# Splitting one step of a token sort in two, in a one-core decoder kernel whose work is interleaved by a planner

## Chip, core and metric

The kernel runs on one core of a Trainium2 chip. The metric is device microseconds of one execution of the whole program; the median of three runs stands for a kernel. A profile is one further execution, recorded by the hardware profiler, with a time of its own.

## What is computed

One decoder layer over x, 4 batches of 512 tokens by 512 channels, in three residual parts:

```
x = x + mamba(layernorm(x))          # in_proj, conv, selective scan over 512 positions, out_proj
x = x + quant_ffn(layernorm(x))      # two int8-style linears, weights given per batch
x = x + moe(layernorm(x))            # 16 experts, each token uses its best 2, and a shared expert
```

The part that is changed belongs to the experts. A router picks two experts for each token; the result is `combine`-weighted:

```
topw, sel = top_k(softmax(x @ gate_w.T), 2)
hmid = silu(einsum('th,eih->tei', x, w1)) * einsum('th,eih->tei', x, w3)
moe_out = einsum('tei,ehi->th', hmid * combine[:, :, None], w2)
```

The kernel does not compute all 16 experts for all tokens. It sorts the tokens by expert into tiles of 128 rows and computes each tile with its one expert.

## The kernel before, in words

**The long work.** The selective scan is cut into 256 units (4 batches of 64), called slots here, counted from 1. `scan_batch` writes one after another. A unit is an exponential on ScalarE (L724), a product on GpSimd (L726), the scan on VectorE (L733) and a product on VectorE (L739, tile `h`, five buffers); TensorE sums `h` over states every few units (L751, into `py`), and VectorE gates the sum (L773).

**The work beside it.** Everything else is written as Python generators that `yield` what their next step needs: an engine's name, a tile, or a condition. `Steps` wraps a generator, and `Pace` keeps a rough plan of when each engine will be free and each tile written. Three times in each unit `more` goes through the generators and lets each do at most two steps; a step is done only if `Pace.clear` agrees. For a step that names PE, the planned end of TensorE's queue may be at most 5,000 ns (`BEHIND`) behind VectorE's, and the tile it names may be ready at most 3,500 ns (`SLACK`) late, each plus the `rest` that the place allows. A bare `yield` names only VectorE and nearly always passes. So a `yield` decides where the instructions after it stand in the engines' queues. The queues themselves are in order: an instruction that waits holds what stands behind it.

**The generators in the last batch of the scan** (slots 193 to 256) are:

- `backs`: for each batch in turn out_proj with its residual (L806, L816), the two quantised linears (transposes and maxima L913, L918; scaling products L963, L974, L1011; products L1081, L1087), and `moe_front`: router (L1197 to L1232) and shared expert (L1147, L1139 up and gate, L1162, then L1171, L1177). Batch 3's part can only start once the scan has ended.
- `routed`, that is `experts` for group 0 (batches 0 and 1): `sort`, then `expert_tiles`.
- after the scan, `last`, which is `experts` for group 1 (batches 2 and 3). From there on the loop at the end of `run` takes the step whose operands the plan has ready first, with 2,000 ns (`FIRST`) in favour of `backs`, or of `last` once the router of batch 3 is done and until its tiles have begun.

**The sort.** T is 8 blocks of 128 tokens, NS is 31 tile places. After counts and positions (L1366 to L1439) a list of token numbers by place is made by products: for each of four pairs of blocks, VectorE writes 0/1 operands `at_r` (L1446) and `at_s` (L1453, L1459), and TensorE adds four small products of them into one PSUM bank `pk` (L1466). After the fourth pair VectorE writes the list `tok` (L1471) and frees the bank. There are three such banks during the scan, a, b and g, for all generators together; eight after it.

**The tiles.** For each tile GpSimd issues two gathers, the rows `xs` (L1505, by `tok`) and the expert's weights `wx` (L1263, by `wrow`). TensorE transposes (L400), ScalarE copies (L1525), TensorE makes the two up-products (L1534), ScalarE and VectorE the gated activation (L1539, L411, L1542), TensorE the down-product (L1547), ScalarE copies (L1550) and SyncE stores the result to `y_d` (L1553). During the scan two tiles are loaded ahead, after it eight. The tiles of a group must be done before the weights of the next are fetched (the condition at L1422, before `first_weights`). At the very end GpSimd gathers `y_d` back by token (L1301), VectorE adds (L1311) and SyncE stores.

Of the kernel before, what the change touches and what calls it, by code (L numbers as in the profile page):

```python
# [46 lines left out]
PE, ACT, POOL, SP = "PE", "Activation", "Pool", "SP"  # L47
# [222 lines left out]
class Kernel:  # L270
# [1083 lines left out]
    def sort(self, sb, G, group, fixed, pos, tok, wrow, count, first_weights, few):  # L1354
# [89 lines left out]
        for t in range(0, T, 2):  # L1444
            at_r = sb.tile([P, 2, 2, P], F16, name="at_r", tag="xT", bufs=few)
            nc.vector.tensor_tensor(  # L1446
                at_r,
                iota_p.rearrange("p (a b q) -> p a b q", a=1, b=1).to_broadcast([P, 2, 2, P]),
                rm[:, t : t + 2, :].unsqueeze(3).to_broadcast([P, 2, 2, P]),
                ALU.is_equal,  # L1450
            )
            at_s = sb.tile([P, 2, 2, NS], F16, name="at_s", tag="ys", bufs=min(2 * few, 6) if few > 2 else few)
            nc.vector.tensor_tensor(  # L1453
                at_s,
                iota_s.rearrange("p (a b q) -> p a b q", a=1, b=1).to_broadcast([P, 2, 2, NS]),
                sl[:, t : t + 2, :].unsqueeze(3).to_broadcast([P, 2, 2, NS]),
                ALU.is_equal,
            )
            nc.vector.tensor_mul(  # L1459
                at_s,  # L1460
                at_s,
                tokf[:, t : t + 2].rearrange("p (a b q) -> p a b q", b=1, q=1).to_broadcast([P, 2, 2, NS]),
            )
            for j in range(2):
                for i in range(2):
                    nc.tensor.matmul(  # L1466
                        pk, at_r[:, j, i, :], at_s[:, j, i, :], start=(t + j + i == 0), stop=(t + j == T - 1 and i == 1)
                    )
            yield
# [338 lines left out]
```

## Time and profile before

| | |
|---|---|
| median of three runs | 1624.45 us (1622.11 to 1625.10) |
| the profiled execution | 1637.25 us, of which the recorded span is 1635.5 us |
| busy share of the span | PE 73%, VectorE 73%, GpSimd 67%, ScalarE 57% |
| mean granted TensorE clock | 0.849 |
| sort of group 0: first operand to `tok` | 1020.7 to 1048.8 us |
| last scan unit ends, its last sum on TensorE ends | 1331.3, 1338.0 us |
| sort of group 1: first operand to `tok` | 1474.8 to 1480.0 us |
| last product of TensorE begins | 1599.0 us |

The profiled execution is 12.8 us longer than the median of the others, so a sum of durations from the profile is set against 1637.25 us and a difference is then carried to the median. In a row of the timeline the columns are start, duration, engine, line, operation, tiles and shapes, and in brackets the idle time before it and what ended it. Each f32 product is recorded as two matmuls, so one line-L1534 step of a tile shows as x16.

### The profile page before, as it was taken

Reading aid. Unit: us, or ns where it says so; the run is one execution under the profiler, and the core shown is the slowest. Engines: PE = TensorE matmul, PEld = TensorE weight load, DVE = VectorE, ACT = ScalarE, POOL = GpSimd, SP = SyncE. Lnnn points to the kernel's source line nnn. Section 1 sums busy time; section 2 is a strip of 40 time slices with the busy share of each in tenths; the row PEclk is TensorE's granted clock in tenths of the full one; section 3 lists DMA queues with packets and bytes.
Section 4 is the critical chain, followed back from the end, with each engine's and each line's share of the span. In section 5 each row is a group of like instructions: output and inputs, shape, how many; then the busy total and the mean of one; then the engine's idle time right before and its main releaser. Section 6 shows DMA issues by size and latency. Waiting matters only on the chain. (4 is left out here: it accounts for less than half of the span.)

```text
span 1635.5 us, 15478 instructions
## 1 busy us (share of the span) xinstructions
PE 1201.9 (73%) x4552; PEld 586.3 (36%) x4552; DVE 1196.0 (73%) x1256; ACT 939.6 (57%) x1592; POOL 1095.3 (67%) x907
## 2 busy tenths in 40 slices
PE   6867877557865767899867885856666799867990
PEld 2222222112332323333423432334434346643670
DVE  4588899898857888788787888977788863453413
ACT  3386677755657778555797753367676413530240
POOL 1079899886768888677887965687878653017443
PEclk9978788768877887999878887888787999978996
DMA  5475555675233655666345559565556557258776
GB/s 200 146 180 128 132 107 118 126 180 119 87 84 73 136 118 157 176 180 166 84 98 118 159 123 280 154 181 129 152 143 186 147 190 258 78 194 304 288 301 233
DMA packets 106521, 262.19 MB, mean 160 GB/s; under 512 B 13056, under 2 KB 17280, under 8 KB 106368
## 3 DMA queue, kind: packets, MB, share of 16 engines
q1 hardware_dynamic: 93120, 204.50, 47.8%
q0 software_dynamic: 13312, 56.63, 9.7%
q8 instruction: 40, 0.66, 0.2%
q14 instruction: 49, 0.40, 0.1%
HBM read 153.87 MB, written 45.88 MB: 122 GB/s over the span
## 5 line engine op out<-in xcount | busy, mean ns | idle before, releaser
L726 POOL TENSOR_TENSOR bu<-bc,rep 128x1024 f32<-128x1024 f32 x256 | 602.0, 2358 | 181.9 <-DVE da L733 135.9
L733 DVE TENSOR_TENSOR_SCAN da<-da,bu 128x1024 f32<-128x1024 f32 x256 | 586.2, 2290 | 89.6 <-POOL bu L726 55.8
L724 ACT ACTIVATE da<-rep,a_sb 128x512 f32<-128x512 f32 x512 | 352.6, 690 | 248.9 <-DVE h L739 221.0
L739 DVE TENSOR_TENSOR h<-da,bc 128x1024 f32<-128x1024 f32 x256 | 312.1, 1219 | 19.4 <-PE py L751 9.1
L751 PE MATMUL py<-h,sel 128*32 128x512 f32 x1024 | 165.1, 683 | 47.7 <-DVE h L739 47.5
L502 POOL TENSOR_TENSOR u<-u,tap 128x511 f32<-128x511 f32 (+2 forms) x72 | 91.1, 1266 | 18.3 <-ACT tap L498 16.0
L446 PE MATMUL bank_a<-xnT,win 128*128 128x512 f32 x176 | 96.5, 699 | 8.9 <-ACT tap L498 6.1
L446 PE MATMUL bank_g<-xnT,win 128*128 128x512 f32 x184 | 89.5, 632 | 5.1 <-ACT tap L498 4.2
L751 PEld LDWEIGHTS py<-h,sel 128*32 128x32 f32 x1024 | 30.9, 117 | 157.8 <-issue 79.9
L1263 POOL DMA_INDIRECT wx<-in_wexp,wrow x48 | 48.9, 1020 | 55.8 <-PE bank L1547 12.3
L446 PE MATMUL bank_b<-xnT,win 128*128 128x512 f32 x120 | 61.1, 656 | 13.0 <-ACT sp_r L681 11.0
L446 PEld LDWEIGHTS bank_a<-xnT,win 128*128 128x128 f32 x176 | 39.1, 230 | 61.3 <-issue 50.1
L1505 POOL DMA_INDIRECT xs<-xn_d,tok x48 | 49.8, 1037 | 16.4 <-issue 14.7
L1301 POOL DMA_INDIRECT yg<-y_d,pos x32 | 32.0, 1002 | 37.3 <-DMA y_d<-ys 21.1
L446 PEld LDWEIGHTS bank_g<-xnT,win 128*128 128x128 f32 x184 | 36.1, 202 | 56.7 <-issue 43.4
L1534 PE MATMUL bank<-xT,wx 128*128 128x128 f32 x368 | 47.4, 284 | 6.7 <-issue 5.3
L695 POOL TENSOR_TENSOR sp_e<-sp_e,dd 128x512 f32<-128x512 f32 x31 | 39.4, 1272 | 16.7 <-ACT dd L690 16.5
L1534 PEld LDWEIGHTS bank<-xT,wx 128*128 128x128 f32 x368 | 45.0, 198 | 10.3 <-issue 8.3
L411 DVE SCALAR_TENSOR_TENSOR hs<-hs,bank 128x128 f32<-128x128 f32 x25 | 7.1, 282 | 52.2 <-ACT hs L1539 45.4
L446 PEld LDWEIGHTS bank_b<-xnT,win 128*128 128x128 f32 x120 | 24.9, 215 | 49.2 <-issue 30.3
L1539 ACT ACTIVATE hs<-bank 128x128 f32<-128x128 f32 x25 | 6.5, 275 | 62.7 <-PE bank L1534 31.5
L806 PE MATMUL bank_g<-wout,u 128*128 128x512 f32 x64 | 34.0, 692 | 10.3 <-ACT tap L498 6.2
(429 smaller groups left out, 2424.2 us busy)
## 6 DMA issues: line engine op xcount, KB each, us to landing
rep<-dd SPq DMA_DIRECT2D x128, 512.0 KB
win<-in_win SPq DMA_DIRECT2D x64, 256.0 KB
x<-xr SPq DMA_DIRECT2D x48, 256.0 KB
xr<-x SPq DMA_DIRECT2D x48, 256.0 KB
y_d<-ys SPq DMA_DIRECT2D x48, 256.0 KB
bc<-rows_d SPq DMA_DIRECT2D x32, 256.0 KB
gz_d<-gz SPq DMA_DIRECT2D x32, 256.0 KB
gzl<-gz_d SPq DMA_DIRECT2D x32, 256.0 KB
```

The source lines that it names most:

```text
L446: nc.tensor.matmul(pj, win[:, k, :], xnT[:, k, :], start=(k == 0), stop=(k == NK - 1))
L502: nc.gpsimd.tensor_add(u[:, j:], u[:, j:], v[j][:, j:])
L695: ew.tensor_sub(e, e, du)
L724: nc.scalar.activation(da[:, i, :], rep[:, i, 0, :], AF.Exp, scale=self.a_sb[:, q, g : g + 1])
L726: nc.gpsimd.tensor_mul(bu, st["bc"][0, g].unsqueeze(1).to_broadcast([P, NP, L]), rep[:, :, 1, :])
L733: self.nc.vector.tensor_tensor_scan(daf, daf, buf, 0.0, ALU.mult, ALU.add)
L739: self.nc.vector.tensor_mul(h, st["da"].pop((c, n)), st["bc"][1, g].unsqueeze(1).to_broadcast([P, NP, L]))
L751: nc.tensor.matmul(py[q * CH : (q + 1) * CH, :], self.sel, st["h"][c, g, q // NP][:, q % NP, :], start=False, stop=(g == NG - 1),)
L806: nc.tensor.matmul(po[t], st["u"][c][:, t * P : (t + 1) * P], wout[c], start=(c == part[0]), stop=(c == part[-1]),)
L1263: nc.gpsimd.indirect_dma_start(out=ws[s], out_offset=None, in_=self.wexp, in_offset=bass.IndirectOffsetOnAxis(ap=wrow[:, s : s + 1], axis= ...
L1505: nc.gpsimd.indirect_dma_start(out=xs[s], out_offset=None, in_=xn_d, in_offset=bass.IndirectOffsetOnAxis(ap=tok[:, s : s + 1], axis=0), bo ...
L1534: nc.tensor.matmul(ph[:, i, :], w[:, o : o + P], xT[:, k, :], start=(k == 0), stop=(k == NK - 1))
```

## The change

In the loop over the four pairs, one `yield` more is put between VectorE's operands and TensorE's products; the one after the products stays. The step that wrote both is now two, and the second is written only when the plan finds TensorE and `at_s` near enough. No instruction is added, removed or altered.

```diff
@@ sort, the loop "for t in range(0, T, 2)", after at_s is written
                 at_s,
                 tokf[:, t : t + 2].rearrange("p (a b q) -> p a b q", b=1, q=1).to_broadcast([P, 2, 2, NS]),
             )
+            yield PE, at_s
             for j in range(2):
                 for i in range(2):
                     nc.tensor.matmul(
```

## Prediction

> **What bounds the kernel now.** I read the page first, then the table of stages by windows, then the waits in the last batch of the scan, then TensorE's own timeline from the end of the scan on, because the change touches two places: a sort that runs beside the scan and one that runs after it. The columns of the windows are stage, length, then busy time and count for PE, PE's weight loads, VectorE, ScalarE and GpSimd, then the granted clock, the DMA share and GB/s.
>
> ```profile
> 1050.00:1338.00 288.00, 203.42 (x915) 113.23 (x913) 231.36 (x232) 171.78 (x301) 209.18 (x174) 0.85 0.55 152
> 1338.00:1444.00 106.00, 92.83 (x502) 63.90 (x502) 42.75 (x102) 45.88 (x99) 25.85 (x39) 0.95 0.50 180
> 1444.00:1480.00 36.00, 21.52 (x85) 14.98 (x86) 21.14 (x77) 8.02 (x12) 12.28 (x19) 0.67 0.65 237
> 1480.00:1526.00 46.00, 40.22 (x116) 20.17 (x116) 14.17 (x23) 3.30 (x7) 27.00 (x28) 0.89 0.82 290
> 1526.00:1600.00 74.00, 70.52 (x461) 54.96 (x459) 17.57 (x52) 29.12 (x67) 31.41 (x31) 1.00 0.78 291
> ```
>
> The first row is the scan beside everything else: VectorE is busy 231 of 288 us and sets the pace, with 57 us of holes. The other rows are the tail: from 1338 to 1444 and from 1526 to 1600 TensorE is the full engine (88% and 95%); the stage between, 1444 to 1480, is a chain of router and sort in which nobody is full. So work moved from the scan into the tail goes from a place where TensorE has 85 us free to one where it has few.
>
> The holes of the scan stage, in the view of who waited for whom (total us, times, longest), and in the groups of that window:
>
> ```profile
> DVE da L733 <- POOL bu L726: 14.9, 6, 5.7
> DVE wsc L974 <- PE bank_b L963: 7.7, 2, 7.4
> L400 PE MATMUL bank_a<-ident,xs 128*128 128x128 f32 x24 | 5.6, 378 | 32.1 <-DMA xs<-xn_d,tok 32.1
> ```
>
> TensorE stood 32.1 us before transposes of tiles whose rows had not come; once this reached VectorE as the 7.4 us hole before L974.
>
> **What the new order is.** The changed program's instruction order per engine can be read without running it. All engines have the same instructions; these stand elsewhere (slots counted as in the text above).
>
> 1. Group 0's sort. Before, the four pairs were written at slots 195, 195, 196, 196 and `tok` at slot 201. Now the first two pairs' operands stand at 195 and 196, and the other two at 204 and 205, because the plan sees the eight-product groups L806 queued on TensorE; `tok` follows at 206. By the starts of L733 (slot 201 at 1046.4 us, 206 at 1069.3) this is about 23 us later. Bank g is held five slots longer, so out_proj of batch 2 alternates a and b alone; its four sums L816 stay at 202, 202, 203, 204, so that costs nothing. What ended up behind: the first two row gathers on GpSimd go from after product 202 to after 207.
> 2. Tiles. The activation L1542 of tile 1 moves from slot 209 to 212, tile 7 from 225 to 235, tile 10 from 235 to 255. Before the scan ended 13 tiles had their L1542, now 10.
> 3. `backs` for batch 2: router from slot 240 to 245, and three of its four last products L1171 used to stand after the last `py` products but one and interleaved with units 254 to 256; now all four stand in one row right before the last L751.
> 4. Group 1's sort: one group L1139 that stood behind the four quads of L1466 now stands before them; on VectorE one L1162 stands before `tok`.
> 5. SyncE's stores L1553 and GpSimd's gathers move with their tiles. In the trace SyncE's queue waited 56 us at L1553 in this stage, in front of `rep` loads L711; with fewer stores there that can only ease, and GpSimd saw `rep` late for just 2.3 us, so I price it at nothing.
>
> **Part 1, the quads themselves.** VectorE's 12 operand instructions take 0.68 + 0.28 + 0.29 us per pair, 1.25 us, four times, before and after; only their slot changes. TensorE's quads take 0.27 us. Before, TensorE stood idle 10.86 us before the first quad with L806 behind it; the first quad is still there, and the second, 0.86 us of waiting, goes. Sum: 0 to -1 us, I take 0.
>
> **Part 2, end of the scan.** From the router of batch 2 to the last L751 TensorE still has in its queue: 12 groups L1147, L1139, L1171 of 3.44 us (start to start in the trace), 41.3; four L751 groups of 1.92, 7.7; three L1534 of 1.79, 5.4; two L1547, two L747 of 0.86, 3.4; two L400 of 0.44, 0.9. That is 58.7 us, nearly without holes since the L1171 wait only for each other's banks; with 3 us for those, 62 us. Before, the same stretch took from 1258.2 to 1338.0, 80 us, of which the five slots that no longer lie in it (L733 of slot 240 at 1255.1, of slot 245 at 1283.5, less the router's own 4.8 us on VectorE) are 24. So 56 us becomes 62: +6 us. Against it stand three tiles' VectorE work no longer in the scan, 3 x 0.57, -1.7 us. I take +4. Bounds: -8 if holes of the scan like the 7.4 us one vanish with the thinner tiles and no new ones come, +9 if new ones come. There is reason for one: the gather of tile 4 now stands behind product 220 on GpSimd and its transpose before the L751 for slots 217 to 220, with four L913 and a VectorE maximum of slot 221 behind; the trace shows 9.3 us from the issue of such a gather to its transpose.
>
> **Part 3, the tail up to 1444.** Of group 0's 24 tiles these steps lay after the last L751 before: 10 L400, 11 L1534, 11 L1547; now 13, 13 and 14. The steps' prices are the distances from start to start in these rows of TensorE's timeline:
>
> ```profile
> 1369.08 1.95 PE L1534 MATMUL bank<-xT,wx 128*128 128x128 f32 x16
> 1370.87 0.60 PE L400 MATMUL bank<-ident,xs 128*128 128x128 f32 x4
> 1371.30 1.88 PE L806 MATMUL bank_a<-wout_c,u 128*128 128x512 f32 x4
> 1373.02 1.02 PE L1547 MATMUL bank_b<-wx,hs 128*128 128x512 f32 x2
> 1373.88 1.02 PE L1547 MATMUL bank_g<-wx,hs 128*128 128x512 f32 x2
> ```
>
> 1.79, 0.43 and 0.86 us: 2 x 1.79 + 3 x 0.43 + 3 x 0.86 = 7.5 us more. Here a rule speaks otherwise. The Trainium skill, "Perfetto Trace Analysis", section "Identifying the Most-Contended Engine", says that matmul busy time misleads on TensorE, and that the share of weight loading tells its slack. That share is 63.9 of 106 us; by it 40% is free and the three tiles cost nothing. The rows decide otherwise: the next group starts exactly where the one before leaves off, whatever loads weights. What the rows do show free is the bracketed holes of the stretch up to the last tile at 1432, 7.5 us in six places, all before steps of the chain or of the tile itself. Not all can be filled, because the holes are waits of 0.6 to 1.9 us; I let tiles fill 3 us. So +4.5 us, between 0 and +7.5. ScalarE and VectorE have half their time free here. DMA moves 180 GB/s here and 290 later, so three tiles' weights find room.
>
> **Part 4, the second sort.** Rows of TensorE's timeline around it:
>
> ```profile
> 1460.26 5.11 PE L1147 MATMUL bank<-xnT,ws 128*128 128x512 f32 x8
> ...
> 1467.02 3.60 PE L1147 MATMUL bank_g<-xnT,ws 128*128 128x512 f32 x8
> 1476.08 0.29 PE L1466 MATMUL bank<-at_s,at_r 128*128 128x31 f16 x4 [5.46 <-DVE at_s L1459]
> 1477.20 0.27 PE L1466 MATMUL bank<-at_s,at_r 128*128 128x31 f16 x4 [0.82 <-DVE at_s L1459]
> ...
> 1479.59 5.69 PE L1139 MATMUL bank_b<-xnT,ws 128*128 128x512 f32 x8
> ```
>
> The hole of 5.46 us now takes an L1139, 3.44 us, which ends before the first `at_s` is there. TensorE's queue is then full from 1479.6 to 1598 as before, one group shorter: -3.4 us. `tok` gets one L1162 before it (0.69 us), but the row gathers stand behind eight weight gathers that GpSimd issues until 1482.7, so that is hidden. The clock could add to it: the L1139 after the holes took 5.69 us and not 3.60. The Trainium skill, "TensorE: Matmul & The Clock Gate", section "HAM oscillation", says that holes of over some 3.4 us let the clock fall; this hole shrinks to 2 us, which by the rule keeps it and saves 2.1 us more. But the granted clock in this stage is 0.67, and the 20 us of layernorm, router and sort around it stay sparse; I take nothing. Bounds -5.5 and 0.
>
> After 1600 nothing changes: sixteen gathers and the last store.
>
> **Sum.** 0 + 4 + 4.5 - 3.4 = +5.1 us on the profiled execution's 1637.25, 1642.3; carried to the median, 1624.45 + 5.1 = 1629.5 us.
>
> **Rivals.**
>
> - *Faster, because TensorE's queue is no longer held by late rows.* Thirteen tiles among the scan cost 32.1 us of TensorE in waits, about 7 us at a time; ten could cost two waits fewer, and each that reaches VectorE is a hole like the 7.4 us before L974. Two such holes less, -14, with parts 3 and 4 as above and +4 at the scan's end: 1624.45 - 14 + 4 + 4.5 - 3.4 = 1615.6. It decides from 6 us of vanished holes on. For it: the first two row gathers now have no L963 of the first linear that waits behind a late one. Against it: the pairs left are spaced just as closely to their transposes. 22%.
> - *No change.* The tail's holes take 6 us of the 7.5, and the scan's end is 2 us later: +2 + 1.5 - 3.4 = 0.1, 1624.6. 15%.
> - *Much slower.* A new hole of 4.5 us at slot 221, the scan's end +6, nothing filled in the tail, and no gain in the sort because bank or operands hold the L1139: 4.5 + 6 + 7.5 = +18, 1642.5. 18%.
> - That the change does nothing is excluded: the order of instructions differs on every engine from slot 196 on.
>
> **Chances.** The likeliest, +2 to +9 us (1626 to 1633), 45%. Within 0.2%, 3.2 us, lies what a measurement here can hardly tell from no change: all of the second rival but a little, and the lower seventh of the likeliest. So faster 0.24, same 0.20, slower 0.56. The range reaches to the faster rival and into the much slower: 1616 to 1645.
>
> **What would show it.** `tok` of group 0 some 20 us later; ten tiles' L1542 before the last L733; the last L751 ending 2 to 6 us later than 1338; 13 up-product groups between it and the second sort; an L1139 in the hole before the first late quad, and the stretch from `tok` to the last product 3 us shorter than 119 us. The prediction is wrong if the scan's end comes over 4 us earlier, that is if the holes of VectorE between 1050 and 1338 sum to well under 57 us, or if the tail from the last L751 to the second `tok` is not longer than its 142 us.

## The result, and the profile after

The changed kernel takes 1637.67 us (median of 12 runs, 1634.24 to 1643.03), the kernel before 1626.01 us in the runs beside it (12 runs, 1622.11 to 1631.79). The ratio is 1.0065, 95% interval 1.0053 to 1.0078: slower, by some 11 us. The prediction had +5.1 us; the sign is right, and 1637.67 lies in the range, but the difference is twice the one forecast. The profiled execution of the changed kernel took 1639.63 us, its span is 1637.9 us. Lines behind the added one are numbered one or two higher in the changed kernels: their L1535 is L1534 of the kernel before.

The two profiled executions differ by 2.4 us only, because that of before had holes on TensorE late in the tail that other profiles do not have (see the last section). For the same reason positions are compared from a common mark: the start of L733 of slot 193, which is the first unit of the last batch. It stands at 994.4 us before and at 993.5 us after. Both kernels were profiled twice.

| us after slot 193 | router L1197 of batch 2 ends | last L733 begins | last sum L751 ends | second list `tok` written |
|---|---|---|---|---|
| before | 263.8 | 334.6 | 343.6 | 485.6 |
| before, second profile | 265.2 | 335.1 | 344.0 | 486.1 |
| after | 277.1 | 336.9 | 354.4 | 504.0 |
| after, second profile | 278.3 | 336.1 | 353.6 | 503.1 |

The last unit of the scan begins 1 to 2 us later. Its last sum on TensorE ends some 10 us later, the second list comes 17 to 18 us later. Such positions vary by some us between executions: group 0's split alone (the first experiment), which has the changed kernel's order up to the second sort, had the last sum at 348.6 and the list at 498.7. From the list on, the last down-product L1547 begins 101.5 us later in both profiles of after. In two kernels that have before's order of work there, and were profiled without those holes (the first and the third experiment), it takes 106.4 and 106.1 us. So 4.6 to 4.9 of the 17 to 18 us come back, which leaves some 13 us where 11 were measured.

The same stretches as windows. First the kernel before; the columns are those of the table of stages (window, length, busy time and count of PE, its weight loads, VectorE, ScalarE, GpSimd, then the granted clock, DMA share and GB/s), the cuts are slot 193, the end of the router, the last sum and the second list:

```profile
994.40:1258.20 263.80, 171.02 (x788) 95.84 (x786) 212.48 (x220) 160.68 (x279) 190.08 (x162) 0.81 0.62 172
1258.20:1338.00 79.80, 67.21 (x248) 30.85 (x247) 67.99 (x76) 28.93 (x48) 49.06 (x39) 0.93 0.52 151
1338.00:1480.00 142.00, 114.36 (x587) 78.87 (x588) 63.89 (x178) 53.90 (x111) 38.13 (x58) 0.88 0.54 194
```

And the changed kernel with the same cuts:

```profile
993.50:1270.60 277.10, 170.47 (x758) 92.52 (x759) 224.81 (x225) 166.67 (x284) 199.53 (x167) 0.77 0.59 161
1270.60:1347.90 77.30, 65.93 (x225) 29.38 (x225) 53.97 (x65) 20.44 (x34) 33.33 (x28) 0.91 0.37 120
1347.90:1497.50 149.60, 123.69 (x643) 85.14 (x647) 66.38 (x186) 57.67 (x119) 44.88 (x65) 0.89 0.59 210
```

The first rows are the finding. Up to the router TensorE is busy for the same time, 171.0 and 170.5 us, but the router ends 13.3 us later: TensorE has stood idle that much longer (106.6 us in place of 92.8; in the second profiles 106.4 and 92.3). The busy time is the same, but the work is not: 758 matmuls in place of 788, with two up-products L1534 fewer, at a granted clock of 0.77 in place of 0.81. VectorE has gone on meanwhile (224.8 against 212.5 us), by four more units of the scan. Whatever TensorE has not done by then is still in front of the second list. The third row shows it arrive: 9.3 us more busy time in 7.6 us more length. Of the 9.3 us, 3.4 are an L1139 that now lies in a hole of the second sort (below) and so adds no length.

What the waits of VectorE name in the stage from 1050 us to the last sum, after (in all, times, longest):

```profile
DVE da L733 <- POOL bu L726: 9.1, 5, 3.4
DVE amx L918 <- PE bank_b L913: 8.9, 2, 6.9
DVE da L733 <- ACT da L724: 8.4, 3, 6.4
DVE xr L816 <- PE bank_a L806: 5.6, 1, 5.6
```

The first of these was 13.3 us in 5 times before; the 14.9 us that the prediction shows are of a window that begins before 1050 us. The 7.4 us hole before L974 of before is gone. In its place are one of 6.9 us before L918, which the prediction had only in its slowest case, with 4.5, and one of 5.6 us before L816, which it had not at all. The holes before transposes for rows that were late have not gone either, as the groups of that window show (32.1 and 6.9 us for banks a and g before):

```profile
L400 PE MATMUL bank_a<-ident,xs 128*128 128x128 f32 x24 | 5.7, 380 | 18.2 <-DMA xs<-xn_d,tok 17.9 <-ACT xn L1017 0.3
L400 PE MATMUL bank_g<-ident,xs 128*128 128x128 f32 x16 | 3.9, 389 | 15.7 <-DMA xs<-xn_d,tok 15.7
```

Three tiles fewer, and 33.6 us of waiting in place of 39.0.

TensorE's timeline at the end of the scan, before, where the last unit began at 1329.0 us:

```profile
1331.24 3.60 PE L1171 MATMUL bank_g<-ws,xn 128*128 128x512 f32 x8
1334.67 0.60 PE L400 MATMUL bank_a<-ident,xs 128*128 128x128 f32 x4
1335.11 1.02 PE L1547 MATMUL bank_b<-wx,hs 128*128 128x512 f32 x2
1336.07 1.92 PE L751 MATMUL py<-h,sel 128*32 128x512 f32 x16
```

And after, where it began at 1330.4 us:

```profile
1330.32 3.60 PE L1171 MATMUL bank_a<-ws,xn 128*128 128x512 f32 x8
1333.76 3.60 PE L1171 MATMUL bank_b<-ws,xn 128*128 128x512 f32 x8
1337.19 3.60 PE L1171 MATMUL bank_a<-ws,xn 128*128 128x512 f32 x8
1340.62 3.60 PE L1171 MATMUL bank_b<-ws,xn 128*128 128x512 f32 x8
1344.06 1.95 PE L1535 MATMUL bank_a<-xT,wx 128*128 128x128 f32 x16
1345.93 1.92 PE L751 MATMUL py<-h,sel 128*32 128x512 f32 x16
```

The last sum begins 15.5 us after the start of the last unit, where it was 7.1 us before: four L1171 and an up-product stand in front of it in TensorE's queue, without a hole between them.

And the second sort, after:

```profile
1483.79 3.60 PE L1147 MATMUL bank_g<-xnT,ws 128*128 128x512 f32 x8
1487.22 3.60 PE L1139 MATMUL bank<-xnT,ws 128*128 128x512 f32 x8
1492.84 0.25 PE L1467 MATMUL bank<-at_s,at_r 128*128 128x31 f16 x4 [2.02 <-DVE at_s L1459]
...
1496.36 5.25 PE L1147 MATMUL bank<-xnT,ws 128*128 128x512 f32 x8
```

The L1139 lies in the hole, which shrinks from 5.46 to 2.02 us. The first group after the quads still takes 5.25 us.

### The profile page after: what moved, and what is told of

The parts are those of the page before. It is cut to its first block, busy times and chain, and to the rows that moved or that the text cites. A ratio compares the mean times of both kernels' runs of the same rounds, so it can differ in the third digit from the quotient of the medians.

```text
span 1637.9 us, 15451 instructions
## 1 busy us (share of the span) xinstructions
PE 1197.6 (73%) x4543; PEld 584.1 (36%) x4552; DVE 1196.1 (73%) x1256; ACT 941.4 (57%) x1592; POOL 1095.3 (67%) x907
## 5 line engine op out<-in xcount | busy, mean ns | idle before, releaser
L733 DVE TENSOR_TENSOR_SCAN da<-da,bu 128x1024 f32<-128x1024 f32 x256 | 586.2, 2290 | 87.4 <-POOL bu L726 50.9
L751 PE MATMUL py<-h,sel 128*32 128x512 f32 x1024 | 166.6, 703 | 43.3 <-DVE h L739 43.1
L751 PEld LDWEIGHTS py<-h,sel 128*32 128x32 f32 x1024 | 31.4, 121 | 157.9 <-issue 88.1
L1506 POOL DMA_INDIRECT xs<-xn_d,tok x48 | 49.4, 1029 | 16.3 <-issue 11.3
L1311 DVE SCALAR_TENSOR_TENSOR xr<-yg,topw,xr 128x512 f32<-128x512 f32 x32 | 23.8, 751 | 28.5 <-DMA yg<-y_d,pos 28.2
L806 PE MATMUL bank_a<-wout,u 128*128 128x512 f32 x64 | 34.6, 701 | 12.1 <-DMA wout<-in_wout 6.2
L395 ACT ACTIVATE xn<-xr,ln_scale 128x512 f32<-128x512 f32 x32 | 25.8, 809 | 26.3 <-POOL ln_scale L391 16.4
L701 POOL TENSOR_TENSOR dd<-dd,u 128x512 f32<-128x512 f32 x31 | 39.4, 1271 | 1.3
```

Of the source, the lines that this page charges most:

```text
L701: ew.tensor_mul(du, delta, st["u"][c])
L733: self.nc.vector.tensor_tensor_scan(daf, daf, buf, 0.0, ALU.mult, ALU.add)
L751: nc.tensor.matmul(py[q * CH : (q + 1) * CH, :], self.sel, st["h"][c, g, q // NP][:, q % NP, :], start=False, stop=(g == NG - 1),)
L1506: nc.gpsimd.indirect_dma_start(out=xs[s], out_offset=None, in_=xn_d, in_offset=bass.IndirectOffsetOnAxis(ap=tok[:, s : s + 1], axis=0), bo ...
```

## The experiments

Three sets of four kernels ran; the kernels of a set share a chip with runs of the kernel before (median 1627.42 us in the first set, 1634.69 in the second, 1626.52 in the third). Differences in us below are the ratio's, on the kernel before of the same set.

**First set: which sort, and what in it.** The added line is kept for one group only.

```diff
+            if group == 0:          # e1: only group 0's sort; e2: "group == 1"
+                yield PE, at_s
```

> The new yield in the first sort (group 0) alone. Its order of instructions up to the second sort is that of the changed kernel. Theory (the loss comes from the first sort's split: TensorE work of the shared expert and of three tiles lands behind the scan's end, about +17 us by the second list, and the second sort's split gives some 3.4 us back): +13 to +16 us against the kernel before, 1640 us. Rival (the second sort's split gives nothing): +11 to +12 us, as the changed kernel. Rival (the loss lies in the second sort): 0.

Measured 1640.72 us, ratio 1.0095 (1.0070 to 1.0121), +15.5 us.

> The new yield in the second sort (group 1) alone; everything up to it stands as in the kernel before, and one L1139 group moves ahead of the quads. Theory: the hole of 5.5 us takes 3.4 us of TensorE work, and TensorE's queue is full from there to its last product: -3.4 us, 1622.6 us. Rival (the stretch after the list is set by the gathers, not by TensorE): 0.

Measured 1621.98 us, ratio 0.9974 (0.9961 to 0.9987), -4.2 us. The two parts are of opposite sign and add up to +11.3 us, the whole within the noise. The split pays in the second sort and costs in the first. The kernel with group 1's split alone is faster than both given kernels.

Next a `yield` that names nothing, in both sorts: two steps, but hardly any gate between them.

```diff
+            yield
```

> The added yield names nothing (no engine, no tile), in both sorts. The step is split just as in the change, but its second half does not ask for TensorE. The list of group 0 is then written at slot 202, one after that of the kernel before, and all tiles stand where they stood. Theory (the condition on TensorE in the plan, not the split, moves the work): 0 us, between -1 and +1. Rival (two steps instead of one use up turns of the planner and so cost by themselves): +5 us or more.

Measured 1631.38 us, ratio 1.0029 (1.0016 to 1.0042), +4.7 us, against an expected zero. The expectation failed, and the trace says why. Up to the second sort the order of instructions is that of the kernel before, but for the list, which stands one unit later, and the names of the banks. L816, which adds out_proj's four sums, before (VectorE's timeline):

```profile
1048.56 0.17 DVE L1471 TENSOR_TENSOR tok<-bank_g,none 128x31 uint32<-128x31 f32 x1
...
1052.68 0.67 DVE L816 TENSOR_TENSOR xr<-xr,bank_a 128x512 f32<-128x512 f32 x1
1053.28 0.68 DVE L816 TENSOR_TENSOR xr<-xr,bank_b 128x512 f32<-128x512 f32 x1
...
1058.31 0.69 DVE L816 TENSOR_TENSOR xr<-xr,bank_g 128x512 f32<-128x512 f32 x1 [1.02 <-PE bank_g L806]
```

and with the bare `yield`:

```profile
1052.80 0.67 DVE L816 TENSOR_TENSOR xr<-xr,bank_a 128x512 f32<-128x512 f32 x1
1053.39 0.18 DVE L1472 TENSOR_TENSOR tok<-bank_g,none 128x31 uint32<-128x31 f32 x1
1053.49 0.68 DVE L816 TENSOR_TENSOR xr<-xr,bank_b 128x512 f32<-128x512 f32 x1
...
1062.92 0.69 DVE L816 TENSOR_TENSOR xr<-xr,bank_a 128x512 f32<-128x512 f32 x1 [5.42 <-PE bank_a L806]
```

The third group of out_proj on TensorE, before and then with the bare `yield`:

```profile
1048.79 9.49 PE L806 MATMUL bank_g<-wout,u 128*128 128x512 f32 x16 [0.55 <-DVE tok L1471]
```

```profile
1053.53 9.36 PE L806 MATMUL bank_a<-wout,u 128*128 128x512 f32 x16 [4.99 <-DVE xr L816]
```

Before, `tok` frees bank g one unit ahead of L816, and out_proj's third group starts in it 0.06 us after the list is written. With `tok` one unit later the third group takes bank a, which the first L816 frees at 1053.5 us; VectorE then stands 5.4 us before the third L816. The changed kernel has the same hole (5.63 us). Counted from slot 193, slot 206 starts 81.0 us on with the bare `yield`, and 75.6 us on with group 1's split alone.

Then the changed kernel with the four L1171 of batch 2 held back until the last sum:

```diff
-            yield PE, xn
+            yield PE, xn, lambda: b != B - 2 or "scanned" in self.done
@@ run, after self.finish(B - 1, 1)
+        self.done.add("scanned")
```

> The changed kernel, but the shared expert's four last products L1171 of batch 2 are held until after the scan's last sums, so that the last L751 no longer stands behind them and an up-product of a tile. Theory A (what counts is how much TensorE work is left when the scan ends; its order there does not matter, since out_proj of batch 3 stands behind all of it): the last L751 ends at 1335 to 1340 instead of 1347.9 in the profile, but the second list comes as late as in the changed kernel, 1497 within 3, and the time stays 1638 us within 3. Theory B (the place of the last sum behind 16 us of other products is the loss): the second list 8 us sooner and 1629 us.

Measured 1632.14 us, ratio 1.0035 (1.0017 to 1.0052), +5.7 us, some 4 to 5 us less than the changed kernel. Between both theories: from slot 193 the last sum ends 341.3 us on, 12 to 13 us sooner, but the list is written 502.3 us on, only 1 to 2 us sooner. The four products take the same time behind the sum as in front of it. That the time gained more than the list did is within the spread of such positions.

**Second set: late pairs, late list, held bank.** All with group 1's sort split; group 0's four pairs are written early, as before.

```diff
-        yield pk
+        yield pk, lambda: group or self.slot >= 207     # e5; e6: 205
```

> Change: group 1's sort split as in the changed kernel; group 0's sort not split, its four pairs written at slots 195 and 196 as before, but its list tok held back until slot 207. By the order of instructions the tiles of group 0 then stand at exactly the slots of the changed kernel (first four activations at 212, 215, 223, 223; ten tiles before the scan's end), and the four last products of batch 2's shared expert stand in one row before the last sum; only the two late pairs are missing. Theory A (the list's lateness and the bank held for it cause the loss, the late pairs themselves nothing): the time of the changed kernel, 1637.7 within 3 us; L816 waits over 4 us in its longest case; last scan unit to last sum 17.5 us, last sum to second list 149 to 150 us. Theory B (the late pairs themselves, which stand between out_proj's products on TensorE and take VectorE's time, cause a part): the hole before L816 stays under 2 us and the time is 1633 to 1634.

Measured 1652.66 us, ratio 1.0098 (1.0068 to 1.0128), +16 us. From slot 193 the router ends 279.8 us on, the last sum 353.2, the list 503.8: the positions of the changed kernel, without its late pairs, and with its hole before L816 (5.48 us). So the late pairs are not needed for the loss, and Theory B falls; a list that comes late, in a bank held for it, is enough. The list is even later here than in the changed kernel, 93.3 us after slot 193 in place of 83.8. (+16 is above the +11 of the changed kernel; the intervals overlap.)

> Change: group 1's sort split; group 0's sort not split, its list held back until slot 205, so that bank g is held nine slots longer than in the kernel before. By the order of instructions the router of batch 2 goes to slot 245 and the activation of tile 1 to 210, but 13 tiles still end before the scan does; after it 16 up-products of tiles are left and not 18. Theory A (it is the held bank that costs at out_proj, and the tiles pushed behind the scan that cost after it): the hole before L816 of 5 us as in the changed kernel, +4 us over the next kernel, which has the same tiles without the held bank; last sum to second list 142.8 - 2 x 1.79 - 0.43 - 0.86 = 138 us; time 1622 - 5 + 4 = 1621. Theory B (a late list delays batch 2 and so the scan's end whatever becomes of the tiles): 1630 or more.

Measured 1636.29 us, ratio 1.0005 (0.9990 to 1.0020).

```diff
         G.done(pk)
-        yield
+        yield lambda: group or self.slot >= 205         # e7: list and bank as before, tiles later
```

> Change: group 1's sort split; group 0's list written at slot 201 and its bank freed as in the kernel before, but the tiles that use it held back until slot 205. Tiles, router and shared expert stand at the same slots as in the kernel with the list held until 205. Theory A: no hole of over 2 us before L816; last sum to second list 138 us; 4.9 us less work after the scan than in the kernel with only group 1's sort split, so 1622 - 5 = 1617 us. Theory B (late tiles cost by themselves): 1626 or more. A third outcome, 1622, would say that what is taken out of the stretch after the scan is paid for within the scan.

Measured 1633.84 us, ratio 0.9991 (0.9977 to 1.0006). Up to the second list the two kernels differ in the place of the first list alone. The hole before L816 follows the bank as expected, 5.0 us in the first of these two and 1.2 us in the second; the times differ by 0.0014 or 2.3 us in the expected direction, but the intervals overlap, so the price of the held bank rests on the bare `yield`. The gain of 5 us against group 1's split alone did not come. The second kernel is rather 0.0017 or 2.8 us slower than that one, with intervals that overlap: the third outcome or a little worse. The windows of the second kernel (tiles from slot 205), with the cuts as above, show how it is paid:

```profile
993.10:1265.60 272.50, 175.69 (x842) 96.28 (x841) 227.26 (x231) 170.46 (x294) 205.97 (x173) 0.78 0.63 176
1265.60:1342.80 77.20, 65.55 (x232) 29.61 (x231) 54.44 (x67) 21.66 (x36) 35.06 (x30) 0.93 0.46 151
1342.80:1478.60 135.80, 112.93 (x562) 75.30 (x559) 63.91 (x178) 52.41 (x107) 36.46 (x57) 0.88 0.52 189
```

The router is 8.7 us later than before here too, again at slot 245. But in that time TensorE did 4.7 us more, and the last stage is 6.2 us shorter. The list stands 485.5 us after slot 193, where it stood before. A late start of the tiles alone thus costs little, if anything. The profiles suggest that what counts is what TensorE gets done until the router; no run changed that alone.

**The kernel before once more.** No edit.

> The kernel before, profiled a second time. If the stretch from the second list to TensorE's last product of 117.9 us was a disturbance of the one profiled execution, it is 105 to 107 us here, and the holes of 1 to 2 us before L1534 between 1504 and 1514 us are gone; if it belongs to the kernel, it is 117 to 118 again. L816's waits on out_proj's products stay under 2 us each in both cases.

Measured 1633.79 us. From the second list to the last down-product it took 114.7 us, neither of the two numbers expected, with a hole of 1.83 us and slow products behind it. That belongs to the last section.

**Third set: three tiles fewer, and better versions.** Group 1's split, and the tiles of group 0 stopped at the tenth until the scan has ended:

```diff
         while ended < likely:
+            if group == 0 and ended == 10:
+                yield lambda: "scanned" in self.done
```

> Change: group 1's sort split, group 0's as in the kernel before, and the tiles of group 0 stopped at the tenth until the scan has ended. By the order of instructions everything up to slot 235 stands as in the kernel with only group 1's sort split (13 tiles done at the scan's end, 0.9974 of the kernel before); after the scan 20 transposes, 20 up-products and 21 down-products are left, as in the changed kernel. This is the changed kernel's shift of three tiles without its late list and its held bank. Theory A (tile work is free beside the scan and costs its price behind it): last sum where it was within 2 us, last sum to second list 149 to 150 us in place of 142.8, the time 7 us over the kernel with only group 1's sort split, 1.001 to 1.002 of the kernel before. Theory B (the scan's last slots give back what three tiles less take from TensorE there, so that the shift costs nothing): last sum 6 us or more sooner, 149 to 150 us after it, the time 0.997 to 0.998 of the kernel before.

Measured 1625.56 us, ratio 0.9998 (0.9989 to 1.0008), 0.0024 or 3.9 us over group 1's split alone, with the intervals of both some 2.6 us. That lies between the theories. Its profile is of the fastest of its 14 runs (1620.98 us). Its windows, cut as above:

```profile
992.90:1257.80 264.90, 173.87 (x786) 97.98 (x786) 212.97 (x220) 161.41 (x280) 190.56 (x162) 0.80 0.62 172
1257.80:1338.60 80.80, 73.21 (x233) 30.93 (x232) 66.91 (x71) 24.39 (x39) 41.05 (x22) 0.97 0.40 112
1338.60:1479.50 140.90, 110.06 (x611) 78.31 (x611) 65.17 (x185) 57.14 (x119) 46.53 (x75) 0.86 0.62 218
```

The same three tiles are behind the scan as in the changed kernel, yet the last stage is 140.9 us long, not 149.6, and the list stands 486.6 us after slot 193. TensorE's timeline tells what took the tiles' place:

```profile
1319.21 1.92 PE L751 MATMUL py<-h,sel 128*32 128x512 f32 x16
1321.06 5.42 PE L806 MATMUL bank_b<-wout_c,u 128*128 128x512 f32 x12
1326.32 5.31 PE L806 MATMUL bank_g<-wout_c,u 128*128 128x512 f32 x12
1331.47 5.31 PE L806 MATMUL bank_b<-wout_c,u 128*128 128x512 f32 x12
1336.71 1.92 PE L751 MATMUL py<-h,sel 128*32 128x512 f32 x16
```

The router being early (264.9 us), the shared expert of batch 2 is done by 1318.4 us, and out_proj of the last batch moves 15.7 us of its work ahead of the last sum. (Not all of batch 3's part has to wait for the end of the scan, as the text on the generators has it: x12 of the x16 of an out_proj group do not need the last units.) In the changed kernel no such work stands there, because the late router left four L1171. So three tiles put behind the scan cost some 4 us by themselves, 1 to 7 with the intervals.

Two tries for a still faster kernel: the hold of the four L1171 on group 1's split alone, and on the kernel with tiles from slot 205.

> Change: group 1's sort split, group 0's as before, and the four last products L1171 of batch 2's shared expert held until the scan's last sum (done to the changed kernel, the same edit took 6 us off). Theory A (TensorE's queue sets the last sum here too): the last sum ends 10 us or more sooner, the stretch from it to the second list is 11 us longer, the time 0.996 of the kernel before or less. Theory B (here VectorE's scan sets the last sum, since only one of the four products stood behind the last units): the last sum ends 4 to 5 us sooner, the stretch after it is 11 us longer, the time 1.001 to 1.002.

Measured 1632.27 us, ratio 1.0038 (1.0021 to 1.0055): 10 us slower than without the hold.

> Change: as the kernel with group 1's sort split and group 0's tiles held back until slot 205 (0.9991 of the kernel before), and the four L1171 of batch 2 held until the scan's last sum; there all four stand before the sums of the last units. Theory A: as in the changed kernel, 6 us less, 0.995 of the kernel before. Theory B (the four products fill time that TensorE has anyway before the last units): 1.001 to 1.003.

Measured 1636.05 us, ratio 1.0059 (1.0042 to 1.0076): 11 us slower than without. Both are worse than Theory B's numbers. In the first the last sum ends 338.7 us after slot 193 (8.9 us sooner than in the profile without the hold), and the stage behind it is 155.6 us long in place of 142.8. So more was added behind the sum (12.8 us) than was saved ahead of it: the four products had in part filled time that TensorE had beside the last units, where its idle time from router to last sum is now 15.5 us in place of 11.4. That is 4 of the 10 us, and more these two profiles cannot show, since their executions differ by 3.8 us: the one without the hold was the slowest of its 22 runs, 3.7 us over their median, the one with it lay 2.8 us under its own. In the second the last sum ends 9 us sooner too, and the stage behind it is 158.6 us long in place of 135.8, so the list comes 13.8 us later. Nothing beat group 1's split alone.

**The changed kernel once more.** No edit.

> The changed kernel again, beside the others on one chip: 1.0065 to 1.0075 of the kernel before. In the stretch from the second list to TensorE's last product, five profiles so far (the changed kernel's among them) had no hole of over 1.1 us and 101 to 106 us, and five (the kernel before's, twice, among them) had holes of 1.1 to 1.8 us before the first up-products after the eight L1147 and L1139 and 112 to 118 us. If these holes belong to the chip and not to the kernel, all four kernels of this set have them or none has.

Measured 1635.78 us, ratio 1.0060 (1.0037 to 1.0083), as before; its positions are in the table above. None of the four kernels of this set had the late holes.

## Why the prediction was right in sign and half in size

**Part 1, the quads and the held bank: mis-sized.** The quads cost nothing that shows, as said: the kernel with the list held until 207 has the positions of the changed kernel without late ones. But "its four sums L816 stay at 202, 202, 203, 204, so that costs nothing" failed. The slots stayed; the third sum's products started a unit later for want of a bank. That is 4.7 us in the kernel with the bare `yield`. It also made the list later than read from before's slots, by 28 to 30 us and not 23. The order of instructions shows where an instruction stands, and not when its bank comes free.

**Part 2, the scan's end: mechanism right, both terms wrong.** The prediction made +6 of a router 24 us later and a stretch to the last sum 18 us shorter (62 for 80), and took +4. Measured, counted from slot 193: the router 13.3 us later, the stretch 2.5 us shorter (77.3 for 79.8), the last sum 10 to 11 us later. The two errors are of opposite sign, so that the forecast came as near as it did is in part luck. The 24 us were taken from before's starts of slots 240 and 245; after, slot 240 begins 5.7 us sooner, and the five units take 23.0 us in place of 28.4. "Nearly without holes" failed: of the 77.3 us TensorE was idle for 11.4, where 3 were allowed, and its busy time was 65.9 us, not 58.7. The groups are those that were counted, but they wait for transfers, and some behind such a wait are slow:

```profile
1282.11 1.09 PE L400 MATMUL bank_g<-ident,xs 128*128 128x128 f32 x4 [5.10 <-DMA xs<-xn_d,tok]
1282.99 6.05 PE L1147 MATMUL bank_b<-xnT,ws 128*128 128x512 f32 x8
...
1299.54 3.67 PE L1147 MATMUL bank_g<-xnT,ws 128*128 128x512 f32 x8 [1.78 <-DMA ws<-in_wexp]
...
1310.46 5.37 PE L1147 MATMUL bank_b<-xnT,ws 128*128 128x512 f32 x8 [2.96 <-DMA ws<-in_wexp]
```

The queue of four L1171 in one row before the last L751 came as read from the order.

**Part 3, the tail: +4.5 forecast, +7.6 measured.** That is the whole price of the three tiles, 7.5 us by the prediction's rows. No tile filled a hole: TensorE's idle time from the last sum to the list went from 27.6 to 25.9 us, and the hole in the sort alone shrank by 3.4. The rows were the better guide than the share of weight loading, 67.91 of 113 us in the window from 1348 to 1461 us, by which the tiles would have been free (the Trainium skill, "Perfetto Trace Analysis", section "Identifying the Most-Contended Engine"). But the ten-tile kernel shows that this is no fixed price of a tile behind the scan: there TensorE had other work to bring forward.

**Part 4, the second sort: right.** -3.4 forecast; -4.2 with group 1's split alone, and -4.6 to -4.9 by the positions. The L1139 is in the hole. No gain of clock was taken, rightly: with a hole of 2.02 us the group behind the quads still took 5.25 us (5.69 before). The rule weighed there (the Trainium skill, "TensorE: Matmul & The Clock Gate", section "HAM oscillation") would have had it at 3.6 us; the measurement decides against it, as far as the longest hole is concerned. In all, TensorE stood idle for 4.7 of the 5.5 us between the L1139 and that group; the granted clock was 0.98 over these 5.5 us and 0.70 in the group.

**The rivals.** Holes did vanish, as the faster rival had it: 7.4 us before L974, and 5.4 us of waiting for rows. New ones, 6.9 us before L918 and 5.6 us before L816, took their place, so it came out on neither side. The case that was called much slower had the right ingredients, the hole at L918 and nothing filled in the tail; against it stood the sort's gain, which it denied.

What is not settled: why the plan moves the router from slot 240 to 245, and why only 8 tiles had their L1542 by slot 245 in the changed kernel where 12 had it with tiles from slot 205. Both come out of the plan's running choices, and no run took these apart. How the +15.5 us of group 0's split divides is known only in part: 4.7 us go with the held bank, some 4 with the three tiles; for the rest TensorE's longer idle time before the router stands, without a run that isolates it.

## What to carry to other kernels

One more point of choice in a generator lets a planner fill a hole in a chain with nothing else to do (here 3.4 us of TensorE's work in the sort behind the scan), and delays what frees a shared bank or starts other work where the engines are full; test the two places apart, since here the half was worth more than the whole. Where an engine's work is fixed and only its order changes, sum its busy and idle time up to each mark: 14 us more of idle time before one mark (92.8 to 106.6) told more than any single hole did. And when the order of instructions says that a step "stays at its slot", ask also whether the buffer that it fills is still free in time.

## What the runs showed of the hardware

All profiles of the second set have holes of one kind, and none of the first and third set has them. The kernel before is slower there too, 1634.69 us in place of 1627.42 and 1626.52. So the holes go with the chip or its hour, and not with the kernel, though no kernel was profiled both with and without them. They come in the first up-products after the eight L1147 and L1139 behind the second list. The kernel before, second profile:

```profile
1503.33 2.84 PE L1534 MATMUL bank<-xT,wx 128*128 128x128 f32 x24
1506.45 0.27 PE L1534 MATMUL bank<-xT,wx 128*128 128x128 f32 x1 [0.28 <-issue]
1508.55 0.38 PE L1534 MATMUL bank<-xT,wx 128*128 128x128 f32 x2 [1.83 <-issue]
...
1510.51 5.29 PE L1171 MATMUL bank_a<-ws,xn 128*128 128x512 f32 x8
```

The products wait for nothing that the profile shows ("issue"), and the next L1171 takes 5.29 us and not 3.60. From the list to the last down-product the four profiles of this set took 112 to 115 us, the nine without such holes 101 to 106. The profile that the prediction started from was of the slow kind (117.9 us), which explains most of the 12.8 us between it and the median of the runs. Such a pair of profiles would have shown +2.4 us for a change that costs 11. What the engine waits for in these holes, no run here tells.
